# Where the low-rank adapters of eight experts are multiplied out: beside the attention scores instead of between other products and in the expert stage

## The chip, the cores and the metric

The kernel runs on one core of a Trainium2 chip. The metric is the device time of one execution in microseconds. The times are medians over several runs; a profile is one further execution, recorded by the hardware profiler.

## The reference

The input is 8 sequences of 512 tokens, 512 wide, in float32. Two layers follow each other, each with attention, a residual and a normalisation, then a feed-forward part, a residual and a normalisation. Only the first layer matters here, and of its feed-forward part the expert weights with their adapters:

```python
# layer 0, attention: 16 heads of 32, causal softmax
scores = jnp.einsum('bhqd,bhkd->bhqk', q, k) * (1.0 / math.sqrt(HD))
attn = jax.nn.softmax(jnp.where(causal, -jnp.inf, scores), axis=-1)
...
# layer 0, feed-forward: 8 experts (E), 2 of them for each token, adapters of rank R = 16
gup = jnp.einsum('th,eho->teo', xf, gate_up_proj)
gup = gup + SCALING * jnp.einsum('ter,eor->teo', jnp.einsum('th,erh->ter', xf, gup_lora_A), gup_lora_B)
gates, h = jnp.split(gup, 2, axis=-1)
h = jax.nn.silu(gates) * h
out = jnp.einsum('tei,eih->teh', h, down_proj)
out = out + SCALING * jnp.einsum('ter,ehr->teh', jnp.einsum('tei,eri->ter', h, down_lora_A), down_lora_B)
```

The adapters need not be applied to the tokens. Before and after, the kernel adds `SCALING * A^T B` to the expert's weights once and uses the sum.

## The kernel before, in words

An expert has six chunks of weights of 128 x 512 (`UPS`): four of gate and up, two of down. All eight experts lie in one SBUF tensor, `experts`. While attention of the first layer runs, the places of experts 4 to 7 hold the attention's own weights and the transposed inputs, so only experts 0 to 3 are loaded early; 4 to 7 follow in the last batch and behind it. The adapters of four experts lie in one tile `lora`, each expert in its own group of 32 partitions, of which 16 are used; the second four take the same tile later.

Attention goes over the batches b = 0 to 7, in each over four groups g of four heads, and in each group over three units u: score columns for key tile 0 (u = 0), key tiles 1 and 3 (u = 1), key tile 2 (u = 2). `scores(b, g, u)` multiplies q and k into the score tile `sc` (4 PSUM banks of 128 x 512, one buffer), ScalarE takes the exponential into `p`, and GpSimd masks the diagonal blocks (`affine_select`). In unit 2 only 256 of each bank's 512 columns are used. One unit later `product` multiplies `p` with the values into `av`, and VectorE adds `p` to the row sums (the line `tensor_tensor(total...)`). A group later, in u = 1, `normalise` sums over the keys (`rs`), takes the reciprocal on VectorE and lets GpSimd add it to a guard (`watch_inverses`, into `g_total`).

Everything else of attention (values, queries, keys, the output projection `ps_o`, the router's logits and choice) is hung between the units by `plan(b)`, as a list of thunks for each (g, u). They share two PSUM banks, the tag `mm`, in turn. The order of instructions on each engine is made by a scheduler at build time from its own estimates; in the last batch from g = 2 on, and in the expert stage's beginning, TensorE's order is the order of the program text. GpSimd also adds a row of biases to the inputs x once per batch (`x + row`), which the scheduler puts near groups 2 and 3.

`merge()` takes the next of 24 steps (e, c), for the experts e and e + 1 and the chunk c. `Experts.merge` multiplies the two deltas (16 rows of contraction, 128 x 512 each) into two `mm` banks named `ps_lora`, ScalarE scales them into `scaled` (two buffers, shared with the reciprocal's tile), and GpSimd adds them to the weights. `plan` places two merges in each of the batches 1 to 6, at (2, 2) and (3, 2) once the block transposes are done by DMA. That makes experts 0 to 3. The other twelve stand behind attention, between the steps of `Tiles` (one step is one tile of 128 tokens through one expert: `gate_up`, `turn_hidden`, `down`), where project, score, choose, dispatch, one_hot and enter of the last batch are placed too.

Of the kernel before, what the change touches and what calls it, by code (L numbers as in the profile page):

```python
# [9 lines left out]
F32 = mybir.dt.float32  # L10
# [4 lines left out]
ALU = mybir.AluOpType  # L15
# [3 lines left out]
P = 128  # L19
NB = 8  # L20
S = 512
D = 512
NT = S // P
ND = D // P
# [734 lines left out]
class Experts:  # L759

    def __init__(self, env, pool):
        self.env, self.nc = env, env.nc
        self.w = pool.tile([P, E * EXPERT], F32, name="experts")
        self.by_expert = self.w.rearrange("p (e f) -> p e f", f=EXPERT)

# [4 lines left out]

    def load(self, e):
        at = e * EXPERT
        for src, n in ((self.env.ins.gate_up[e], ND), (self.env.ins.down[e], UPS - ND)):
            self.nc.sync.dma_start(out=self.w[:, at : at + n * 512].rearrange("p (u f) -> p u f", f=512),
                                   in_=src.rearrange("u p f -> p u f"))
            at += n * 512
# [4 lines left out]
        for j in range(4):  # L783
            self.nc.sync.dma_start(out=self.lora[32 * j : 32 * j + R, :], in_=self.env.ins.lora[i, j])

    def delta(self, ps, e, c):
        j = 32 * (e % 4)
        a, bt = lora_factors(self.lora[j : j + R, :], c)
        self.nc.tensor.matmul(ps, lhsT=a, rhs=bt, start=True, stop=True)

    def chunk(self, e, c, n=1):
        return self.by_expert[:, e : e + n, 512 * c : 512 * (c + 1)]

    def merge(self, e, c, ps, scaled):


        for i in range(2):
            self.delta(ps[i], e + i, c)
        for i in range(2):
            self.nc.scalar.mul(scaled[i], ps[i], LORA_SCALE)  # L800
            w = self.chunk(e + i, c)[:, 0, :]
            self.nc.gpsimd.tensor_tensor(w, w, scaled[i], ALU.add)


class Tiles:
# [425 lines left out]
def attention0(env, guard, keep, routes, experts, dram, p_mm, tiles_ctx):  # L1231
# [8 lines left out]
    with ExitStack() as phase:  # L1240
# [151 lines left out]
        def scores(b, g, u):  # L1392
            q, k = heads[b, g]
            sc = p_sc.tile([P, 4, S], F32, tag="sc", name="sc")
            width = 0
            for kt in UNITS[u]:
                w = S - P * kt
                for j in range(4):
                    hs = slice(HD * j, HD * (j + 1))
                    matmul_by_columns(nc, sc[:, j, width : width + w], k[hs, ts(kt, P)], q[hs, P * kt :], columns=64)  # L1400
                width += w
            p = own.tile([P, 4, width], F32, tag=f"p{u}", name="p", bufs=2 if u == 0 else 1)
            nc.scalar.activation(p, sc[:, :, :width], AF.Exp, scale=scale)  # L1403

            at = 0
            for kt in UNITS[u]:
                first = p[:, :, at : at + P]
                nc.gpsimd.affine_select(out=first, in_=first, pattern=[[0, 4], [1, P]], compare_op=ALU.is_ge, fill=0.0,  # L1408
                                        base=0, channel_multiplier=-1)
                at += S - P * kt  # L1410
            return p

        def product(b, g, u, p, acc):
# [28 lines left out]
            nc.vector.tensor_tensor(aoTs[b][:, g, :], av, r_inv, ALU.mult)  # L1442
            guard.watch_inverses(r_inv)

        merges = [(e, c) for e in range(0, E, 2) for c in range(UPS)]

        def merge(n=1):
            for _ in range(min(n, len(merges))):
                e, c = merges.pop(0)
                ps = [mm([P, 512], "ps_lora") for _ in range(2)]  # L1450
                experts.merge(e, c, ps, [work.tile([P, 512], F32, tag="r_inv", name="scaled", bufs=2) for _ in ps])

        def plan(b):

            todo, late = ({(g, u): [] for g in range(ND) for u in range(len(UNITS))} for _ in range(2))
            for slot, places in (((0, 0), (0, 1)), ((0, 1), (3,)), ((0, 2), (2,))):
                todo[slot] += [lambda t=t: value(b, t) for t in places]
            pb, last = b - 1, b == NB - 1
            by_dma = 0 <= pb < by_blocks
            for g in range(ND):  # L1460
                nb, ng = (b, g + 1) if g + 1 < ND else (b + 1, 0)
                if nb < NB:
                    todo[g, 0 if by_dma and ng == 0 else 1].append(lambda nb=nb, ng=ng: query(nb, ng))
                    todo[g, 1 if by_dma and ng == 0 else 2].append(lambda nb=nb, ng=ng: key(nb, ng))
            if b:
                places = ((1, 0), (1, 1), (1, 2), (2, 0)) if by_dma else ((1, 0), (1, 0), (1, 1), (1, 1) if last else (1, 2))
                for t, slot in enumerate(places):
                    todo[slot].append(lambda t=t: project(pb, t))
                if by_dma:
                    todo[2, 1].append(lambda: blocks(pb))  # L1470
                else:
                    for c in range(ND):
                        at = todo[2, 1] if last and c >= 2 else (late if last else todo)[2, 0]
                        at.insert(c % 2 if at is todo[2, 1] else len(at), lambda c=c: turn(pb, c))
                todo[(3, 2) if by_dma else (2, 1)].append(lambda: score(pb))
                if not by_dma:
                    todo[2, 2].append(lambda: choose(pb))
                if not last:
                    todo[2, 2 if by_dma else 1].append(merge)
                    todo[3, 2 if by_dma else 1].insert(0, merge)  # L1480
            if b == 0:
                todo[1, 0].append(lambda: router.merge_lora(mm([P, ND, E], "ps_wr")))
            if b > 1:
                todo[0, 0].append(lambda: choose(b - 2))
                todo[1, 0].append(lambda: dispatch(b - 2))
                todo[1, 2].append(lambda: enter(one_hot(b - 2, range(NT))))
            if last:
                todo[1, 2].append(soon)
                todo[2, 2].append(first_rows)
                late[3, 1].append(first_turned)  # L1490
                todo[3, 2] += [begin, lambda: dispatch(b - 1)]
            return todo, late
# [25 lines left out]
        for b in range(NB):  # L1518
            todo, late = plan(b)
            for g in range(ND):  # L1520
                if g == 2:
                    if b + 1 < NB:
                        load_xT(b + 1)

                    nc.gpsimd.tensor_tensor(xs[b], xs[b], row[:, 1:2, :].to_broadcast([P, NT, D]), ALU.add)
                if g == 3 and b + 1 < NB:
                    load_x(b + 1)
                if b == NB - 1 and g == 1:
                    experts.load_lora(work, 1)
                    experts.load(4)  # L1530
                if b == NB - 1 and g == 2:
                    order.enter_context(in_order(tc))
                if b == NB - 1 and g == 3:
                    experts.load(5)
                    experts.load(6)
                acc = []
                for u in range(len(UNITS)):
                    p = scores(b, g, u)
                    for thunk in todo[g, u]:
                        thunk()  # L1540
                    begun.close()
                    if waiting is not None:
                        waiting()
                    for thunk in late[g, u]:
                        thunk()
                    if u == 1 and summing is not None:
                        summing()
                    waiting = lambda b=b, g=g, u=u, p=p, acc=acc: product(b, g, u, p, acc)
                summing = lambda b=b, g=g, acc=acc: normalise(b, g, acc)
        waiting()  # L1550
        summing()
        merge()
        heads_ctx.close()
        tiles.open(tiles_ctx)
        tiles.step(merge)
        b = NB - 1
        one_hot(b - 1, (0, 1))
        project(b, 0, True)
# [5 lines left out]
        enter(rows, columns=P)  # L1564
        for _ in range(2):
            tiles.step()
            merge()
        for c in range(ND):
            turn(b, c, mm if c in (1, 2) else tiles.aside)
        tiles.step()  # L1570
        score(b)
        merge()
        choose(b, P)
        tiles.step()
        merge()
        dispatch(b, tiles.aside, P)
        for places in ((0, 1), (2, 3)):
            rows = one_hot(b, places)
            tiles.step()
            merge()  # L1580
        enter(rows, tiles.aside, P)
        tiles.of_fixed = router.fixed(routes)
        while merges:
            tiles.step()
            merge()
        order.close()
    return router, tiles, router.tables(routes, p_mm.tile([P, E], F32, tag="mm", name="ps_count"), guard.routed[:, 1:2])

# [289 lines left out]
def usual_pass(tc, ins, held_out):  # L1878
    nc = tc.nc
    with ExitStack() as ctx:  # L1880
# [4 lines left out]
        with tc.tile_pool(name="a_mm", bufs=2, space=PSUM) as p_mm, ExitStack() as attn1_ctx:  # L1885
            with tc.tile_pool(name="routes", bufs=1, side="right") as routes, \
                    tc.tile_pool(name="experts", bufs=1, side="right") as pool, ExitStack() as tiles_ctx:
                experts = Experts(env, pool)
                router, tiles, tables = attention0(env, guard, keep, routes, experts, dram, p_mm, tiles_ctx)

                def load_rows(b):
# [335 lines left out]
```

## Time and profile before

| | |
|---|---|
| median of 3 runs | 2159.9 us (2158.47 to 2159.97) |
| profiled execution | 2158.07 us, of which the span of instructions is 2156.4 us |
| mean granted TensorE clock | 0.997 |
| TensorE busy | 2121.3 us (98% of the span) |
| VectorE busy | 1280.0 us (59%) |
| ScalarE busy | 628.8 us (29%) |
| GpSimd busy | 495.0 us (23%) |
| attention of layer 0 | about the first 700 us of the span |
| expert tiles | from about 696 us to about 1150 us |

Busy time counts an engine's instructions, not its waits. Work on the other engines counts only where TensorE ends up waiting for it. In a timeline a line has the start in us, the length, the engine, the line of the kernel, the operation, what it writes and reads, how often it came in a row, and in brackets the idle time before it with what ended it. A float32 product appears as two records, one for each pass.

### The profile page before, as it was taken

The page shows a single profiled execution, that of the slowest core. Times are in us where ns is not written, and L with a number is a line of the kernel's source. Part 1 is how long each engine was busy: PE and PEld are TensorE (multiplying, and loading weights), DVE is VectorE, ACT ScalarE, POOL GpSimd, SP SyncE. Part 2 cuts the span into 40 slices and gives each one's busy share as a digit, 9 for nine tenths or more (in the row PEclk, how much of TensorE's full clock was granted, in tenths as well). Part 3 has the DMA queues.
Part 4 walks back from the last instruction along what each step waited for, and adds up shares of the span by engine and source line. Part 5 has one row for each costly group of instructions (what it writes and reads, how often), then busy time and mean ns, then how long its engine had stood idle before and what let it go on. Part 6 is the DMA issues. An engine that isn't in the chain of part 4 may idle for free. (4 is left out here: it accounts for less than half of the span.)

```text
span 2156.4 us, 35260 instructions
## 1 busy us (share of the span) xinstructions
PE 2121.3 (98%) x14746; PEld 996.3 (46%) x14746; DVE 1280.0 (59%) x2042; ACT 628.8 (29%) x907; POOL 495.0 (23%) x489
## 2 busy tenths in 40 slices
PE   9999999999998999999999999999999999999997
PEld 2333333333333444444443333333334888888886
DVE  2657676776767544224326988889857644555443
ACT  2332323323323221122124333332332232222222
POOL 2333414424233342132014222232211000000000
PEclk9999999999999999999999999999999999999999
DMA  9030312303222228797644121331201311111000
GB/s 308 21 95 6 99 30 71 99 2 98 71 68 89 98 91 231 214 234 195 193 157 139 57 87 55 98 98 40 79 1 45 103 59 59 59 59 59 20 20 21
DMA packets 160010, 195.53 MB, mean 91 GB/s; under 512 B 61010, under 2 KB 101970, under 8 KB 157282
## 3 DMA queue, kind: packets, MB, share of 16 engines
q1 hardware_dynamic: 148560, 157.49, 23.8%
q0 software_dynamic: 10560, 34.61, 5.6%
q8 instruction: 119, 1.95, 0.4%
q10 hardware_dynamic: 722, 1.07, 0.1%
q14 instruction: 49, 0.40, 0.1%
HBM read 123.67 MB, written 69.47 MB: 90 GB/s over the span
## 5 line engine op out<-in xcount | busy, mean ns | idle before, releaser
L911 PE MATMUL ps_gu<-experts,xrT 128*128 128x512 f32 (+1 forms) x520 | 247.4, 598 | 0.0
L1403 ACT ACTIVATE p<-sc 128x2048 f32<-128x2048 f32 (+1 forms) x96 | 153.1, 1595 | 144.8 <-PE sc L62 121.1
L1165 DVE SCALAR_TENSOR_TENSOR hT<-ps_u,vec,sg 128x512 f32<-128x512 f32 x88 | 65.6, 746 | 189.4 <-PE ps_u L1160 189.4
L1176 PE MATMUL ps_f<-ffn_w,h_half 128*128 128x512 f32 x672 | 169.7, 393 | 2.7 <-DVE h_half L1171 2.0
L1015 POOL TENSOR_TENSOR g_total<-g_total,r_inv 128x512 f32<-128x512 f32 x64 | 90.0, 1406 | 352.4 <-DVE r_inv L1788 270.2
L1408 POOL TENSOR_SCALAR_AFFINE_SELECT p<-p 128x512 f32<-128x512 f32 x128 | 90.2, 717 | 341.0 <-ACT p L1403 303.5
L1431 DVE TENSOR_TENSOR p<-p 128x1536 f32<-128x1536 f32 (+2 forms) x96 | 139.3, 1451 | 44.6 <-POOL p L1408 41.2
L1758 ACT ACTIVATE p<-sc 128x1024 f32<-128x1024 f32 x128 | 124.1, 1022 | 99.0 <-PE sc L62 98.9
L913 DVE TENSOR_TENSOR h<-ps_gu,h 128x256 f32<-128x256 f32 x67 | 28.5, 425 | 207.0 <-ACT h L912 207.0
L1788 DVE RECIPROCAL r_inv<-r_inv 128x512 f32<-128x512 f32 x32 | 107.1, 3346 | 68.5 <-ACT r_inv L1012 68.5
L1176 PEld LDWEIGHTS ps_f<-ffn_w,h_half 128*128 128x128 f32 x672 | 124.4, 188 | 34.9 <-DVE h_half L1171 7.7
L1160 PE MATMUL ps_g<-x_high,ffn_w 128*128 128x512 f32 x352 | 137.2, 390 | 0.9 <-DVE x L1730 0.9
L1160 PE MATMUL ps_g<-x_low,ffn_w 128*128 128x512 f32 x352 | 137.0, 389 | 0.0
L911 PEld LDWEIGHTS ps_gu<-experts,xrT 128*128 128x128 f32 x520 | 95.6, 196 | 89.5 <-issue 89.2
L1160 PE MATMUL ps_u<-x_high,ffn_w 128*128 128x512 f32 x352 | 136.9, 389 | 0.0
L1160 PE MATMUL ps_u<-x_low,ffn_w 128*128 128x512 f32 x352 | 136.9, 389 | 0.0
L927 PE MATMUL ps_y<-experts,hT 128*128 128x512 f32 (+1 forms) x272 | 128.0, 593 | 0.5 <-ACT hT L921 0.5
L62 PE MATMUL ps_q<-experts 128*32 128x512 f32 x1024 | 121.9, 605 | 4.9 <-DMA experts<-in_xT 4.6
L62 PE MATMUL sc<-qT,kT 64*64 64x512 f32 x1024 | 124.7, 602 | 1.1 <-ACT qT L1664 0.7
L1777 PE MATMUL av<-p,v 128*64 128x512 f32 x512 | 120.9, 593 | 0.0
L62 PE MATMUL ps_o<-attn_out,aoT 128*64 128x512 f32 x512 | 116.4, 598 | 0.8 <-ACT r_inv L1012 0.8
L62 PE MATMUL ps_k<-experts 128*32 128x512 f32 x1024 | 116.3, 594 | 0.0
(269 smaller groups left out, 3275.8 us busy)
## 6 DMA issues: line engine op xcount, KB each, us to landing
results<-y SPq DMA_DIRECT2D x68, 256.0 KB, 2.2
turned<-turned SPq DMA_DIRECT2D x56, 256.0 KB, 4.1
pair<-xrT SPq DMA_DIRECT2D x25, 512.0 KB, 3.1
xrT<-pair SPq DMA_DIRECT2D x100, 128.0 KB, 4.5
x<-in_x SPq DMA_DIRECT2D x8, 1024.0 KB, 8.3
experts<-in_gate_up SPq DMA_DIRECT2D x8, 1024.0 KB, 11.4
rows<-x SPq DMA_DIRECT2D x32, 256.0 KB, 2.3
x<-rows SPq DMA_DIRECT2D x8, 1024.0 KB, 15.4
```

What stands on the lines that cost most here:

```text
L62: nc.tensor.matmul(out[m], lhsT=lhsT[:, m], rhs=rhs, start=start, stop=stop)
L911: nc.tensor.matmul(ps, lhsT=xT[:, c, :], rhs=self.weights(i, c), start=c == 0, stop=c == ND - 1)
L927: self.nc.tensor.matmul(ps, lhsT=hT[:, c, :], rhs=self.weights(i, ND + c), start=c == 0, stop=c == self.NI - 1)
L1015: self.nc.gpsimd.tensor_tensor(self.total, self.total, r_inv, ALU.add)
L1160: nc.tensor.matmul(ps, lhsT=w[:, ts(dc, P)], rhs=x[:, dc, :], start=(dc, i) == (0, 0), stop=(dc, i) == (ND - 1, 1))
L1176: self.nc.tensor.matmul(os[t], lhsT=h[:, ts(t, P)], rhs=self.weights(2 * NHID + c), start=(c, i) == (0, 0), stop=(c, i) == (NHID - 1, 1))
L1403: nc.scalar.activation(p, sc[:, :, :width], AF.Exp, scale=scale)
L1408: nc.gpsimd.affine_select(out=first, in_=first, pattern=[[0, 4], [1, P]], compare_op=ALU.is_ge, fill=0.0, base=0, channel_multiplier=-1)
L1431: nc.vector.tensor_tensor(total[:, :, P * kt :], total[:, :, P * kt :], p[:, :, at : at + w], ALU.add)
L1758: nc.scalar.activation(p, sc, AF.Exp, scale=scale)
L1777: nc.tensor.matmul(st["av"][HD * j : HD * (j + 1), :], lhsT=st["v"][:, kt, HD * j : HD * (j + 1)], rhs=p[:, j, :], start=kt == 0, stop=kt ...
L1788: nc.vector.reciprocal(r_inv, r_inv)
```

## The change

1. The deltas are made four experts at a time, for one chunk's half (256 columns), in columns of 64: eight small products per time. They are written into the 256 columns of each bank of `sc` that unit 2 does not use, just ahead of unit 2's scores. This is done in all four groups of batches 1 to 6, 24 times. Batches 1 to 3 make experts 0 to 3, batches 4 to 6 make experts 4 to 7.
2. ScalarE scales them two experts at a time, straight behind the exponential, into tiles of their own. GpSimd's add follows one unit later for the first pair and two units later for the second.
3. For experts 4 to 7 the weights' half chunks are loaded for this purpose, added to, and stored to a DRAM tensor `merged`. In the last batch and behind it, those experts are loaded from `merged`, one transfer each.
4. The second adapters are loaded at the start of batch 4 instead of in batch 7.
5. All calls of `merge` go. The loop at the end that ran a step for each merge left now runs until twelve steps are done.
6. The area for descriptors of GpSimd's own DMAs is set to 8192 bytes a partition.

```diff
+    def deltas(self, ps, c, half):
+        for e in range(4):
+            a, bt = lora_factors(self.lora[32 * e : 32 * e + R, :], c)
+            matmul_by_columns(self.nc, ps[:, e, :], a, bt[:, 256 * half : 256 * (half + 1)], columns=64)
+    def pair(self, ps, i, k, own):
+        nc = self.nc
+        second, c, half = k // 12, k % 12 // 2, k % 2
+        e, f = 2 * i, slice(512 * c + 256 * half, 512 * c + 256 * (half + 1))
+        scaled = own.tile([P, 2, 256], F32, tag=f"scaled{i}", name="scaled")
+        nc.scalar.mul(scaled, ps[:, e : e + 2, :], LORA_SCALE)
+        if not second:
+            w = self.by_expert[:, e : e + 2, f]
+            return {1 + i: lambda: nc.gpsimd.tensor_tensor(w, w, scaled, ALU.add)}
+        w = []
+        def load():
+            w.append(own.tile([P, 2, 256], F32, tag=f"merged{i}", name="merged"))
+            ins, u = self.env.ins, c if c < ND else c - ND
+            src = (ins.gate_up if c < ND else ins.down)[4 + e : 6 + e, u, :, 256 * half : 256 * (half + 1)]
+            nc.sync.dma_start(out=w[0], in_=src.rearrange("e p f -> p e f"))
+        return {i: load, 1 + i: lambda: nc.gpsimd.tensor_tensor(w[0], w[0], scaled, ALU.add),
+                2 + i: lambda: nc.sync.dma_start(out=self.merged[:, e : e + 2, f], in_=w[0])}
...
     def load(self, e):
         at = e * EXPERT
+        if e >= 4:
+            self.nc.sync.dma_start(out=self.by_expert[:, e, :], in_=self.merged[:, e - 4, :])
+            return
...
         def scores(b, g, u):
             q, k = heads[b, g]
             sc = p_sc.tile([P, 4, S], F32, tag="sc", name="sc")
+            free = sc[:, :, S - 256 :]
+            beside = ND * (b - 1) + g if u == 2 and 0 < b < NB - 1 else None
+            if beside is not None:
+                experts.deltas(free, beside % 12 // 2, beside % 2)
...
             nc.scalar.activation(p, sc[:, :, :width], AF.Exp, scale=scale)
+            n = len(UNITS) * (ND * b + g) + u
+            if beside is not None:
+                for i in range(2):
+                    for after, thunk in experts.pair(free, i, beside, own).items():
+                        merging.setdefault(n + after, []).append(thunk)
...
+            for thunk in merging.pop(n, []):
+                thunk()
             return p
...
-                if not last:
-                    todo[2, 2 if by_dma else 1].append(merge)
-                    todo[3, 2 if by_dma else 1].insert(0, merge)
...
+                if b == NB // 2 and g == 0:
+                    experts.load_lora(work, 1)
                 if b == NB - 1 and g == 1:
-                    experts.load_lora(work, 1)
                     experts.load(4)
...
-        while merges:
+        while tiles.next < 12:
             tiles.step()
-            merge()
...
-    nc = bacc.Bacc("TRN2", target_bir_lowering=False, num_devices=1)
+    nc = bacc.Bacc("TRN2", target_bir_lowering=False, num_devices=1, dynamic_dma_scratch_size=8192)
```

More of the change, by code (lines that the diff above doesn't have):

```diff
@@ L759, with __init__ @@
 class Experts:
-    def __init__(self, env, pool):
+    def __init__(self, env, pool, dram):
         self.env, self.nc = env, env.nc
+        self.merged = dram.tile([P, 4, EXPERT], F32, name="merged")
         self.w = pool.tile([P, E * EXPERT], F32, name="experts")
@@ L784, in load_lora @@
             self.nc.sync.dma_start(out=self.lora[32 * j : 32 * j + R, :], in_=self.env.ins.lora[i, j])
[L786 to L802, printed above, removed]
+    def deltas(self, ps, c, half):
[19 more added lines that the diff above has]
+                2 + i: lambda: nc.sync.dma_start(out=self.merged[:, e : e + 2, f], in_=w[0])}
 class Tiles:
@@ L1443, in normalise @@
             guard.watch_inverses(r_inv)
[L1445 to L1451, printed above, removed]
+        merging = {}
         def plan(b):
@@ L1551, in attention0 @@
         summing()
-        merge()
         heads_ctx.close()
         tiles.open(tiles_ctx)
-        tiles.step(merge)
+        tiles.step()
         b = NB - 1
@@ L1566, in attention0 @@
             tiles.step()
-            merge()
         for c in range(ND):
@@ L1571, in attention0 @@
         score(b)
-        merge()
         choose(b, P)
         tiles.step()
-        merge()
         dispatch(b, tiles.aside, P)
@@ L1579, in attention0 @@
             tiles.step()
-            merge()
         enter(rows, tiles.aside, P)
         tiles.of_fixed = router.fixed(routes)
-        while merges:
+        while tiles.next < 12:
             tiles.step()
-            merge()
         order.close()
@@ L1887, in usual_pass @@
                     tc.tile_pool(name="experts", bufs=1, side="right") as pool, ExitStack() as tiles_ctx:
-                experts = Experts(env, pool)
+                experts = Experts(env, pool, dram)
                 router, tiles, tables = attention0(env, guard, keep, routes, experts, dram, p_mm, tiles_ctx)
```

## The prediction

> **What bounds the kernel now.** I read the page's busy table first, then the answers on the tile ps_lora (the products of the adapters, which the change moves), then the timelines of TensorE, VectorE and GpSimd around the places where they stand.
>
> ```profile
> PE 2121.3 (98%) x14746; PEld 996.3 (46%) x14746; DVE 1280.0 (59%) x2042; ACT 628.8 (29%) x907; POOL 495.0 (23%) x489
> L789 PE MATMUL ps_lora<-lora x96: 587/640/692, 148.6 to 799.6; 16*128 16x512 f32 x96
> 140.00:700.00 560.00, 22.69 (x52) 7.60 (x52) 14.94 (x25) 1.00 0.22 70
> 700.00:820.00 120.00, 13.16 (x44) 3.58 (x44) 12.76 (x23) 0.99 0.33 109
> ```
>
> TensorE is busy for 98% of the span, so time is won only where its own work goes or where one of its waits goes. The 96 records are 48 products, two passes each. The last two lines are that tile's busy time (PE, weight load, ACT): 22.69 us in the attention batches, 13.16 us in the tail (experts' first tiles). So at most about 36 us is at stake. The seam between two batches, on TensorE (start, length, group, idle before it):
>
> ```profile
> 249.54 0.69 PE L62 MATMUL sc<-q,k 32*64 32x256 f32 x16
> 250.16 1.44 PE L789 MATMUL ps_lora<-lora 16*128 16x512 f32 x4
> 252.03 1.06 PE L498 MATMUL ps_logits<-x1T,r_wr 128*32 128x512 f32 x8 [0.43 <-ACT scaled L800]
> 252.91 1.05 PE L1423 MATMUL av<-p,v 128*32 128x384 f32 x16
> 253.88 1.11 PE L62 MATMUL sc<-q,k 32*64 32x512 f32 x16
> 254.93 7.07 PE L62 MATMUL ps_v<-experts 128*32 128x512 f32 x64
> 261.82 0.44 PE L62 MATMUL ps_r<-r_gather,logits 128*32 128x8 f32 x31
> ```
>
> A merge of two products costs 252.03 - 250.16 = 1.87 us of TensorE here, a wait of 0.43 us on ScalarE in it. The other engines at the same seam:
>
> ```profile
> 245.14 4.57 POOL L1525 TENSOR_TENSOR x<-x,row 128x2048 f32<-128x2048 f32 x1 [0.99 <-issue]
> 251.42 1.57 POOL L1408 TENSOR_SCALAR_AFFINE_SELECT p<-p 128x512 f32<-128x512 f32 x1 [0.53 <-ACT p L1403]
> 255.91 1.54 POOL L1015 TENSOR_TENSOR g_total<-g_total,r_inv 128x512 f32<-128x512 f32 x1 [1.67 <-DVE r_inv L1441]
> 257.40 2.26 POOL L802 TENSOR_TENSOR experts<-experts,scaled 128x512 f32<-128x512 f32 x1
> 252.43 3.34 DVE L1441 RECIPROCAL r_inv<-r_inv 128x512 f32<-128x512 f32 x1
> 256.83 1.70 DVE L1431 TENSOR_TENSOR p<-p 128x1024 f32<-128x1024 f32 x1
> 258.64 0.69 DVE L1307 TENSOR_TENSOR v<-ps_v,row 128x512 f32<-128x512 f32 x1
> ```
>
> See that unit 2's mask (251.42) comes before g_total, that VectorE's sum of that unit (256.83) is long since free to run, and that the first v leaves its bank (258.64 to 259.33) 2.5 us before ps_r, which takes that bank, starts at 261.82.
>
> **Removed in the batches.** Each of batches 1 to 6 has two merges: 1.87 us above, and 237.16 - 235.23 = 1.93 us in group 2. 6 x 3.80 = 22.8 us. Two waits of ps_v on ScalarE's scaled copy go too (1.3 us in the list of waits). Together -24.1 us.
>
> **Added in the batches.** 24 times, eight products of 16 x 64 by 16 x 256, written to the half of the score tile that unit 2 leaves unused. The trace has no such group, but sc of unit 2 has the same number of instructions, column halves, width, row groups and banks: 250.16 - 249.54 = 0.62 us. I assume 16 rows are no quicker than 32, and two row groups do overlap with 16 rows: a ps_lora merge takes 1.06 us in the tail (702.14 to 703.20) against 1.93 us where it can't. Bounds 0.6 and, if only two ran at once, 16 records at about 0.24 us over 2, 1.9 us. I take 0.62: 24 x 0.62 = +14.9 us.
>
> **Waits that the change makes.** The order built for each engine shows two.
> (1) Score tile. It has one buffer; its release now waits for exp (1.02 us) and two scaled copies (1.09 us the pair, 0.60 us each). I set before and after equal at the start of rs in group 2 (230.07). After: sc of unit 2 in group 3 starts at 248.73, ends 249.42, exp 249.52, copies end 251.65, sc of the next batch may start about 251.85. TensorE's own work until then (logits 0.88, av 0.98, one v instruction 0.22) ends at 251.43. Wait 0.42 us. In groups 0 to 2 a key (3.46) and av (0.98) stand there: hidden.
> (2) GpSimd's order. The new order puts g_total ahead of unit 2's mask, and both adds right behind that mask. g_total waits for VectorE's reciprocal, so the mask slips behind it. At the seam: reciprocal ends 255.7, g_total 257.35, mask (0.63) 258.0, first add (1.27) 259.25, then VectorE's sum (1.15 undisturbed: 256.83 plus 1.70, less the wait for g_total's end at 257.4), v's evacuation at 260.5 to 261.2. ps_r would start at 251.85 + 1.05 + 6.68 = 259.58. Wait about 1.6 us.
>
> Does the sum wait for one add, for both, or for none? Row: the add at 257.40 takes 2.26 us and not 1.27, since the sum was waiting when g_total ended and went first. [...] If VectorE won at once it would be 0.35 us; if it lost twice, 2.9 us. [...]
>
> In groups 0 to 2 the same slip has cover: o needs v's bank at 196.0 and gets it at about 195.7; o in group 1 at 221.3, about 220.1; in group 2 the mask is done at 240.7 and its av starts at 241.2. These are thin, 0.3 to 1.2 us. x + row (245.14) waits for its load and in batch 4 came 1.3 us later; that goes straight into the seam: +1.3 us once. Sum of waits: 6 x 2.0 + 1.3 = +13.3 us. Ends: 6 x 0 and 6 x 4.2.
>
> **Batches:** -24.1 + 14.9 + 13.3 = +4.1 us.
>
> **The tail.** Twelve merges go: 1.99 (696.30), ten of 1.06, 1.87 (744.09): 14.46 us, and 0.15 us of ps_x1T on scaled. But the merge at 744.09 hid ScalarE's copy of the logits:
>
> ```profile
> 743.10 1.06 PE L498 MATMUL ps_logits<-x1T,r_wr 128*32 128x512 f32 x8
> 744.09 1.90 PE L789 MATMUL ps_lora<-lora 16*128 16x512 f32 x4
> 745.96 1.06 PE L62 MATMUL ps_r<-r_gather,logits 128*128 128x8 f32 x8
> 746.87 3.66 PE L911 MATMUL ps_gu<-experts,xrT 128*128 128x512 f32 x4
> 745.00:750.00 5.00, 5.00 (x15) 0.70 0.18 52
> ```
>
> The copy ends at 744.82, so ps_r now waits 0.86 us. The next late thing would be the last project: its VectorE chain (one-hots) was held for 4.33 us by GpSimd's g_total and two adds; without the adds it ends near 708, ps_o needs its bank at 709. -14.6 + 0.86 = -13.75 us.
>
> The last line is the granted clock: 0.70 over these 5 us, and the four ps_gu at 746.87 took 3.66 instead of 1.88 us. TensorE was never idle; 3.8 us of thin products stood before. [...]
>
> **Edits taken at nothing.** 48 transfers of 256 KB on SP's queue (24 loads, 24 stores) and the second adapters' load moved from batch 7 to 4: SP mostly waits for VectorE's normalised rows, the DMA engines are 0.17 to 0.26 busy there, and the adapters have a unit of 20 us. A late store would hold x's load behind it, at the price of the batch-4 case: 0 to 1.3 us a batch in 4 to 6. Experts 4 to 7 now come in one load each; needed at tile 12. The smaller descriptor area: no row shows it; an indirect DMA takes GpSimd 0.96 us and is issued five tiles ahead; 0 to 3 us, I take 0.
>
> **Sum.** +4.1 - 13.75 - 1.75 = -11.4 us against the profiled execution's 2158.07 us (its span is 2156.4): 2146.7. The median of the runs, 2159.9, is 1.8 us above that execution: 2148.
>
> **Rivals.**
> - No new waits (0.14): VectorE wins its turns and the score tile is free in time. -24.1 + 14.9 - 15.5 = -24.7: 2135. For it: GpSimd is 23% busy. Against: the order on GpSimd.
> - Slower, the adds hold VectorE (0.10): both adds go ahead of each sum. Then o in group 0 waits 0.9 us, ps_r 2.9, the score tile 0.42, and thin covers in groups 1 and 2 about 0.8: 5.0 a batch, 30 us instead of 13.3, and the dip stays: 2148 + 16.9 + 1.75 = 2167. It decides from (24.1 - 14.9 + 15.5)/6 = 4.1 us a batch on. For it: the 4.33 us row, where VectorE lost twice running. Against: in all twelve adds behind a g_total VectorE went first.
> - The change doesn't do what it says (0.06): the eight products don't overlap, 1.9 instead of 0.62 us, 24 x 1.28 = 31 us more: 2179.
>
> **How the numbers follow.** The forecast has 0.70, with 2141 to 2156 as its own range. With the rivals, 2137 to 2158 leaves about 2 in 10 out. A measurement of this kernel tells 0.2% (4.3 us, so 2155.6 and 2164.2) from no change. Faster: 0.14 and nine tenths of 0.70, about 0.78; same: the rest of 0.70 and a share of the slower rival, 0.11; slower: 0.11.
>
> **What would show it.** Right: no ps_lora; sc groups from lora of 0.62 us; at each seam sc waits about 0.4 us on ScalarE and ps_r 1 to 2 us on VectorE; in the tail steps of 5.8 instead of 7.06 us; clock 1.00 after ps_logits. Wrong: lora groups above 1 us; waits above 4 us a batch; a late x; stalls of TensorE after 850 us.

## The result, and the profile after

The changed kernel takes 2143.07 us (median of 6 runs, 2142.19 to 2145.68), the kernel before 2159.87 us in the same session. The ratio is 0.9928, 95% interval 0.9918 to 0.9938: faster by 16.8 us, where 11.4 to 11.9 us were forecast (2148, range 2137 to 2158). The profiled execution is the longest of the six (2145.68 us, span 2143.9) and the one of before lay 1.8 us under its median, so the two traces differ by 12.5 us in span. The reckoning below is one of traces; the differences of medians stand beside it.

The page's busy line, and the answer on the tile lora (the products that took the place of ps_lora):

```profile
PE 2099.9 (98%) x15034; PEld 992.5 (46%) x15034; DVE 1283.9 (60%) x2042; ACT 627.3 (29%) x907; POOL 498.1 (23%) x489
L62 PE MATMUL sc<-lora x384: 374/400/426, 100.1 to 597.3; 16*64 16x256 f32 x192
```

TensorE has more instructions and is busy for 21 us less. The timeline of TensorE at the seam that was shown of before (start, length, group, and in brackets the idle time ahead of it and who ended it):

```profile
247.92 1.04 PE L1462 MATMUL rs<-p,ones 128*32 128x512 f32 x8
248.89 0.69 PE L62 MATMUL sc<-lora 16*64 16x256 f32 x16
249.38 0.64 PE L62 MATMUL sc<-q,k 32*64 32x256 f32 x16
249.94 1.07 PE L498 MATMUL ps_logits<-x1T,r_wr 128*32 128x512 f32 x8
252.57 1.07 PE L1447 MATMUL av<-p,v 128*32 128x384 f32 x16 [1.56 <-POOL p L1430]
253.46 1.02 PE L62 MATMUL ps_v<-experts 128*32 128x512 f32 x2
254.41 1.11 PE L62 MATMUL sc<-q,k 32*64 32x512 f32 x16
255.46 7.07 PE L62 MATMUL ps_v<-experts 128*32 128x512 f32 x62
263.24 0.44 PE L62 MATMUL ps_r<-r_gather,logits 128*32 128x8 f32 x32 [0.72 <-DVE v L1320]
```

Four things are to be seen.

- The group of lora delays the scores behind it by 249.38 - 248.89 = 0.49 us, not 0.62.
- ps_r waits for VectorE as forecast, but 0.72 us (six times, 4.3 us in the list of waits), not 1.6.
- av, which was ready to run in the forecast, waits 1.56 us for a mask on GpSimd: five times, 4.7 us in all.
- The score tile's wait on ScalarE does not appear. Two records of ps_v, the two passes of one product, stand ahead of the next scores instead, and this is not free: by themselves they hold TensorE for 254.41 - 253.46 = 0.95 us, and the 62 behind them take 7.07 us, as the 64 did before.

GpSimd and VectorE at the same place:

```profile
247.37 4.56 POOL L1540 TENSOR_TENSOR x<-x,row 128x2048 f32<-128x2048 f32 x1 [2.08 <-DMA x<-in_x]
251.86 1.24 POOL L1430 TENSOR_SCALAR_AFFINE_SELECT p<-p 128x512 f32<-128x512 f32 x2
258.13 1.54 POOL L1028 TENSOR_TENSOR g_total<-g_total,r_inv 128x512 f32<-128x512 f32 x1 [5.02 <-DVE r_inv L1465]
259.62 0.63 POOL L1430 TENSOR_SCALAR_AFFINE_SELECT p<-p 128x512 f32<-128x512 f32 x1
260.23 3.49 POOL L805 TENSOR_TENSOR experts<-experts,scaled 128x512 f32<-128x512 f32 x2
252.55 2.17 DVE L1455 TENSOR_TENSOR p<-p 128x1536 f32<-128x1536 f32 x1 [8.34 <-POOL p L1430]
254.64 3.34 DVE L1465 RECIPROCAL r_inv<-r_inv 128x512 f32<-128x512 f32 x1
260.28 2.30 DVE L1455 TENSOR_TENSOR p<-p 128x1024 f32<-128x1024 f32 x1 [1.17 <-POOL p L1430]
```

x + row begins when x has landed, holds GpSimd until 251.9, and only then come the two masks that av waits for (252.57). The sum behind unit 2's mask takes 2.30 us, where the prediction reckoned 1.15 for the sum alone and one add of 1.27 ahead of it: that part is as forecast.

TensorE in the tail, and a window of 5 us (the granted clock is the number after the five engines' busy times, here 1.00):

```profile
731.82 2.10 PE L1374 MATMUL ps_x1T<-ident,x 128*128 128x128 f32 x16 [0.94 <-DVE xrT L900]
...
739.65 1.06 PE L498 MATMUL ps_logits<-x1T,r_wr 128*32 128x512 f32 x8
741.43 1.06 PE L62 MATMUL ps_r<-r_gather,logits 128*128 128x8 f32 x8 [0.71 <-ACT logits L1387]
742.34 1.96 PE L924 MATMUL ps_gu<-experts,xrT 128*128 128x512 f32 x4
...
749.34 0.41 PE L62 MATMUL ps_rank<-both,r_before 128*128 128x32 f32 x2 [0.94 <-DVE xrT L900]
...
762.61 1.91 PE L62 MATMUL ps_table<-one_hot 128*128 128x256 bf16 x16 [0.94 <-DVE xrT L900]
745.00:750.00 5.00, 4.06 (x16) 2.11 (x15) 3.65 (x18) 1.67 (x2) 0.00 (x0) 1.00 0.09 35
```

The clock is 1.00 behind ps_logits and the four ps_gu take 1.96 us: the dip is gone. ps_r waits 0.71 us, as reckoned. Three waits of 0.94 us are new and were not forecast: ps_x1T, ps_rank and ps_table use the bank of the ps_xrT just before them, and a merge used to stand between.

By anchors in the two traces: up to ps_r of the last batch (675.72 before, 676.93 after) the change loses 1.2 us; from there to the end (1480.6 against 1466.9 us) it gains 13.7.

### The profile page after: what moved, and what is told of

It reads as the page before. It is cut to its first block, busy times and chain, and to the rows that moved or that the text cites. A ratio compares the mean times of both kernels' runs of the same rounds, so it can differ in the third digit from the quotient of the medians.

```text
span 2143.9 us, 35859 instructions
## 1 busy us (share of the span) xinstructions
PE 2099.9 (98%) x15034; PEld 992.5 (46%) x15034; DVE 1283.9 (60%) x2042; ACT 627.3 (29%) x907; POOL 498.1 (23%) x489
## 5 line engine op out<-in xcount | busy, mean ns | idle before, releaser
L1455 DVE TENSOR_TENSOR p<-p 128x1536 f32<-128x1536 f32 (+2 forms) x96 | 149.3, 1555 | 80.6 <-POOL p L1430 77.5
L62 PE MATMUL ps_v<-experts 128*32 128x512 f32 x1024 | 120.9, 594 | 0.0
L1430 POOL TENSOR_SCALAR_AFFINE_SELECT p<-p 128x512 f32<-128x512 f32 x128 | 81.5, 649 | 165.3 <-ACT p L1420 158.7
```

The lines of the kernel that those rows point to most:

```text
L62: nc.tensor.matmul(out[m], lhsT=lhsT[:, m], rhs=rhs, start=start, stop=stop)
L1455: nc.vector.tensor_tensor(total[:, :, P * kt :], total[:, :, P * kt :], p[:, :, at : at + w], ALU.add)
```

## The experiments

All ratios are to the kernel before, run beside them. "Period" is the length of a batch in the profiled execution: the mean of the five distances between the six starts of ps_logits between about 160 and 605 us (the six seams).

| kernel | median us | ratio (95%) | period us |
|---|---|---|---|
| before | 2159.87 | 1 | 86.87 |
| changed | 2143.07 | 0.9928 (0.9918 to 0.9938) | 87.06 |
| tail_left_out | 2142.67 | 0.9927 (0.9913 to 0.9941) | 86.66 |
| nothing_merged | 2127.11 | 0.9858 (0.9843 to 0.9873) | 83.89 |
| products_only | 2140.12 | 0.9911 (0.9896 to 0.9926) | 86.07 |
| no_adds | 2138.42 | 0.9906 (0.9891 to 0.9921) | 85.85 |
| x_row_moved | 2147.01 | 0.9943 (0.9929 to 0.9956) | 88.53 |
| x_row_in_reciprocal | 2142.73 | 0.9930 (0.9917 to 0.9944) | 85.59 |
| before_x_moved | 2158.48 | 1.0000 (0.9991 to 1.0009) | 86.59 |
| tail_banks | 2139.78 | 0.9911 (0.9898 to 0.9925) | 86.98 |
| both_moves | 2138.62 | 0.9906 (0.9891 to 0.9921) | 85.63 |
| both_moves_2 | 2133.89 | 0.9889 (0.9874 to 0.9904) | 85.58 |

### Where the gain sits: tail_left_out

```diff
 # in the kernel before
                 e, c = merges.pop(0)
+                if len(merges) < 12:
+                    return
                 ps = [mm([P, 512], "ps_lora") for _ in range(2)]
```

> The kernel before, with the twelve merges of the tail left out (half of the adapters are then not added); the batches are untouched. It tells how the gain divides. Theory T (the tail made all of it): from the profiled executions the tail is 13.7 us shorter after the change and the batches 1.2 us longer, so this kernel should take 13 to 15 us off the kernel before (about 2146 us, ratio 0.9935), with three new waits of ps_x1T, ps_rank and ps_table on VectorE's copy of the turned rows (0.94 us each), one of ps_r on ScalarE's logits (0.7 us), and the granted clock at 1.00 after ps_logits. Rival B (the batches gave part of it): the medians differ by 16.8 us where the profiled executions differ by 12.4; if the rest sits in the tail, 17 us or more come off here, and if the batches gave 3 us, 13 to 14 come off.

It took 2142.67 us, 16 us under the before of its session (2158.63) and level with the changed kernel: the gain is the tail's, and the batches give about nothing. In the trace the stretch from the last batch's ps_r to the end is 1466.6 us, 14.0 less than before, with the same three waits of 0.94 us and the clock at 1.00 from 735 to 750. Theory T. The interval of the ratio is 12.7 to 18.8 us, so a few us from the batches (rival B) are not excluded by the medians; the periods, 86.66 here and 87.06 in the changed kernel, speak against any.

### What the parts cost in the batches: nothing_merged, products_only, no_adds

```diff
 # nothing_merged: no products, and none of the rest
-            if beside is not None:
-                experts.deltas(free, beside % 12 // 2, beside % 2)
 # nothing_merged and products_only: no copies, adds, transfers
-            if beside is not None:
-                for i in range(2):
-                    for after, thunk in experts.pair(free, i, beside, own).items():
-                        merging.setdefault(n + after, []).append(thunk)
         # in load(): experts 4 to 7 come from gate_up and down, as in the kernel before
 # no_adds
-            return {1 + i: lambda: nc.gpsimd.tensor_tensor(w, w, scaled, ALU.add)}
+            return {}
-        return {i: load, 1 + i: lambda: nc.gpsimd.tensor_tensor(w[0], w[0], scaled, ALU.add),
-                2 + i: lambda: nc.sync.dma_start(...)}
+        return {i: load, 2 + i: lambda: nc.sync.dma_start(...)}
```

> The changed kernel without the merging: no products, copies, adds or transfers of merged weights (the adapters are not added). Against products_only it prices the 24 groups of eight products. By the trace a group delays what follows by 0.48 us: 24 x 0.48 = 11.5 us, of which those at the seams may be hidden in the wait of av; so 9 to 12 us less than products_only, about 2127 us. The prediction had 0.62 us each, 14.9 us. Rival: products of 16 rows run wholly beside the scores: no difference.

> The changed kernel with the 24 groups of adapter products in the score tile alone: no scaled copies, no adds, no load or store of merged weights (the adapters are not added). Against the run without adds it tells what the two scaled copies cost through the score tile's release. Theory S of the prediction (release late by 0.42 us at each seam): 2 to 3 us less than without adds, about 2136 us. Rival (hidden, since av waits there longer or as long): no difference, 2138 us; the transfers of merged weights delaying x would show here too, as less wait of av on the mask in batches 4 to 6.

> The changed kernel without its 48 adds on GpSimd (the adapters are then not added; products, scaled copies, loads and stores stay). Theory A (the first add holds VectorE's sum behind the mask): the sum of unit 2 takes 1.15 us instead of 2.30 at each seam, the first v leaves its bank 1.15 us earlier and the wait of ps_r (0.72 us) goes: 4 to 5 us less than the changed kernel, about 2139 us. Theory X (x + row sets the seam): the same for ps_r, but av's wait on the mask stays at 0.4 to 1.6 us in the seams. [...]

From nothing_merged to products_only the period grows by 86.07 - 83.89 = 2.18 us, four groups at 0.55; 13.0 us in the medians. Copies and transfers of merged weights add nothing on balance (85.85 - 86.07 = -0.22): the rival of theory S. But this is a balance of two things. In no_adds, as in the changed kernel, the two records of ps_v stand ahead of the next scores and cost 0.95 us a seam; in products_only they do not, so the late release of the score tile shows as another order and not as a wait. In their place ps_r waits for VectorE at each of the six seams of products_only, 5.3 us in all, with no add on GpSimd:

```profile
253.05 7.07 PE L62 MATMUL ps_v<-experts 128*32 128x512 f32 x64
261.00 0.44 PE L62 MATMUL ps_r<-r_gather,logits 128*32 128x8 f32 x32 [0.88 <-DVE v L1317]
```

The adds bring 87.06 - 85.85 = 1.21 us; 4.7 us in the medians, as theory A had it. VectorE and TensorE at the seam of no_adds:

```profile
257.99 1.63 DVE L1454 TENSOR_TENSOR p<-p 128x1024 f32<-128x1024 f32 x1 [1.16 <-POOL p L1429]
259.54 1.44 DVE L1319 TENSOR_TENSOR v<-ps_v,row 128x512 f32<-128x512 f32 x2
250.28 1.07 PE L1446 MATMUL av<-p,v 128*32 128x384 f32 x16 [0.79 <-POOL p L1429]
260.27 0.44 PE L62 MATMUL ps_r<-r_gather,logits 128*32 128x8 f32 x32
```

The sum takes 1.63 instead of 2.30 us and ps_r no longer waits. av still waits for the mask, but less: 1.1 us in two seams instead of 4.7 in five. So A and X do not divide the two waits between them. Both waits hang on one chain: x + row, masks, VectorE's sum and reciprocal, g_total, mask, sum, v. The adds make it longer, x + row makes it start late, and taking away either is enough for ps_r: it no longer waits in x_row_moved (below), with all adds in place. (Part of av's wait also differs from one execution to the next: tail_banks below, with the same attention, has 2.9 us of it.)

The surprise is nothing_merged. Taking the two merges out of a batch of tail_left_out saves 86.66 - 83.89 = 2.8 us, not the 3.8 us that they took. The list of waits of nothing_merged says where the rest went (us in all, times, the longest):

```profile
PE av L1438 <- POOL p L1421: 6.1, 6, 1.3
```

With nothing at all in the merge's place av waits for the mask at every seam. So this wait is not made by what the change adds; it appears when the merge goes. Nor is it made by the changed order on GpSimd: here unit 2's mask runs ahead of g_total, as before.

### Who holds the masks: x_row_moved, x_row_in_reciprocal, before_x_moved

```diff
 # x_row_moved
-                    nc.gpsimd.tensor_tensor(xs[b], xs[b], row[:, 1:2, :].to_broadcast([P, NT, D]), ALU.add)
                     p = scores(b, g, u)
+                    if (g, u) == (1, 0):
+                        token = row[:, 1, 0:1]
+                        nc.vector.scalar_tensor_tensor(out=token, in0=p[:, 0, 0:1], scalar=0.0, in1=token, ...)
+                        for t in range(NT):
+                            nc.gpsimd.tensor_tensor(xs[b][:, t, :], xs[b][:, t, :], row[:, 1, :], ALU.add)
 # x_row_in_reciprocal: the same four adds in normalise() for g == 0, after
+                nc.scalar.activation(token, guard.sums[:, n : n + 1], AF.Identity, scale=0.0, bias=token)
```

The token (a zero times something that is ready at the wanted time, added to one element of row) only holds the four pieces back.

> The changed kernel, with GpSimd's x + row of each batch (4.56 us, one instruction, which stands between two masks just before the seam as soon as x has landed) held back to the next batch's second group and cut in four pieces. Theory X (GpSimd's x + row sets the seam): the masks of unit 1 at the seam come up to 4 us earlier, TensorE's waits of av on the mask (4.7 us in five seams) go, VectorE's reciprocal comes earlier with them, so ps_r's waits (4.3 us) go as well; seams fall from 14.6 us to about 11.9 on average, 12 to 16 us in all: about 2128 us. Rival A (the two adds between mask and sum set ps_r, as the prediction had it): av's waits go, the seam loses 0.8 us, ps_r still waits 0.7 us or more: 2138 us. Rival N: x lands later or the pieces meet the masks of the other group: no gain or a loss.

The seams (start of rs to start of ps_r) fell from between 13.85 and 15.32 us to 11.82 (the first to 12.39), 11.9 on average as theory X had it, and the waits of av and ps_r are gone from the list. A part of this only changed places: four records of ps_r now start ahead of the last three of ps_v, and the others 0.84 us later:

```profile
348.54 0.27 PE L62 MATMUL ps_r<-r_gather,logits 128*32 128x8 f32 x4
348.95 0.60 PE L62 MATMUL ps_v<-experts 128*32 128x512 f32 x3
349.38 0.42 PE L62 MATMUL ps_r<-r_gather,logits 128*32 128x8 f32 x27
```

And the kernel as a whole gained nothing: the period is 1.5 us longer than in the changed kernel, the median 4 us higher (with its five runs between 2142.77 and 2150.09). The rest of a batch rose from 72.6 to 77.05 us, 3.6 more without those 0.84. VectorE's routing, the wait on TensorE and the windows (clock before the last two columns) of x_row_moved:

```profile
284.17 4.99 POOL L1559 TENSOR_TENSOR x<-x,row 128x512 f32<-128x512 f32 x4 [0.28 <-DVE row L1556]
285.55 1.17 DVE L562 TENSOR_TENSOR mine<-r_part,r_hots 128x32 f32<-128x32 f32 x1
288.11 1.08 DVE L566 CAST rank<-r_ranks 128x8 int32<-128x8 f32 x1
295.33 0.74 DVE L1331 TENSOR_SCALAR q<-ps_q,vec 128x512 f32<-128x512 f32 x1
296.13 1.07 PE L1462 MATMUL rs<-p,ones 128*32 128x512 f32 x8 [1.88 <-DVE q L1331]
298.51 4.94 PE L62 MATMUL ps_k<-experts 128*32 128x512 f32 x32
297.00:300.00 3.00, 3.00 (x44) 0.99 (x44) 3.00 (x3) 2.04 (x4) 0.00 (x0) 0.63 0.02 5
```

Beside the pieces, an operation of VectorE on 128x32 that takes 0.18 us in the changed kernel takes 1.17, and one on 128x8 1.08 instead of 0.17; q leaves its bank late, rs waits 1.88 us, and behind this wait the clock is 0.63, so that ps_k takes 4.94 instead of 3.64 us. The adds were put into a hole of GpSimd that was no hole of VectorE.

> The changed kernel, with x + row (in four pieces) held back until ScalarE has read the row sums in the next batch's second group, so that GpSimd runs it while VectorE computes a reciprocal (3.3 us, one operand) and no longer beside VectorE's routing chain. Theory X (x + row held the seam, and where it was put last it held VectorE's routing, which made rs wait 1.9 us and the TensorE clock drop): seams stay at 11.8 us, the rest of a batch goes back from 77.0 to about 72.6 us, the clock stays at 1.00: 6 x 2.8 = 17 us less than the changed kernel, about 2126 us. Rival (x + row costs some 4 us a batch wherever GpSimd runs it, since VectorE's sums with two operands wait for it): the rest stays above 75 us and the time near 2145 us.

The seams stayed at 11.82, rs waited no more, the period fell to 85.59. The rest of a batch (73.8) looks 1.2 us longer, 0.84 of it because of the same change of places at ps_r. Yet the median did not move. At the sixth ps_r (600.95) the trace is 9.8 us ahead of the changed kernel's (610.75); the last batch takes 5.9 of them back (72.1 us to the next ps_r against 66.2), and its ps_x1T waits 4.2 us for VectorE instead of 1.6. That x + row's place in that batch did it is what both_moves_2 shows below. The other 4 us are still there at the end of the trace (span 2140.4 against 2143.9) but not in the medians; the changed kernel's traced execution was the longest of its six.

> The kernel before with x + row held back in the same way as in both_moves_2 and nothing else. It tells whether the merge at the seam had covered x + row. Theory C (it had: TensorE spent the 1.87 us of the merge while GpSimd ran x + row and the masks behind it, so before nothing of it was on the path): the seams fall from 13.5 us only to 13.25, 0 to 3 us less in all, about 2157 us, or a loss where x + row now holds VectorE. Rival (x + row cost the kernel before as much as the changed one): 9 us or more less, below 2150 us.

The edit of both_moves_2 (below), without its tail, in the kernel before: ratio 1.0000, interval 0.9991 to 1.0009, all six seams 13.25 us. In the kernel before x + row cost nothing but its late arrivals, and the same edit is worth about 1.5 us a batch in the changed one. Together with nothing_merged this shows that the merges had covered x + row: theory C. Both of a batch's merges seem to have had a part in it: the merge at the seam held av back, and the one in group 2 held rs back while x + row waited for its own load. At the seam shown x + row starts 248.57 - 245.14 = 3.4 us ahead of rs in the kernel before, 1.5 us in nothing_merged and 0.55 us (247.92 - 247.37) in the changed kernel.

### The tail's new waits, and a better kernel: tail_banks, both_moves, both_moves_2

```diff
-            turn(b, c, mm if c in (1, 2) else tiles.aside)
+            turn(b, c, tiles.aside if c == 2 else mm)
-        dispatch(b, tiles.aside, P)
+        dispatch(b, mm, P)
-        enter(rows, tiles.aside, P)
+        enter(rows, columns=P)
```

> The changed kernel, with three products of the tail in the other pool of PSUM banks (the first ps_x1T, ps_rank and ps_table), so that they do not ask for the bank of the ps_xrT just before them. Theory W (each of them waited 0.94 us for VectorE's copy of ps_xrT, which a merge had hidden before): three waits go, 2.8 us less than the changed kernel, about 2140 us. Rival: the products then wait for the bank's earlier user or the next ps_xrT waits for ps_x1T, and nothing is gained.

It took 2139.78 us, 3 us less; the three waits left the list. TensorE in tail_banks, in the place of the second one:

```profile
744.06 0.60 PE L899 MATMUL ps_xrT<-ident,xr 128*128 128x128 f32 x4
744.50 0.31 PE L62 MATMUL ps_rank<-both,r_before 128*128 128x32 f32 x2
```

> The changed kernel with both moves: x + row held back as in x_row_in_reciprocal, and the three products of the tail in the other bank pool as in tail_banks. If the two are independent the gains add up: 17 us of the seams and 3 us of the tail, about 2123 us, 36 us below the kernel before. Rival: if x + row costs the same wherever it runs, only the tail's 3 us are left, about 2140 us.

2138.62 us: the tail's gain and about 1 us more, the last batch (71.3 us) being nearly as long as in x_row_in_reciprocal. The expected sum was missed for that reason, and both_moves_2 mends it:

```diff
 # x + row in normalise()
-            if g == 0:
+            if g == 0 and b < NB - 1:
 # and for the last batch where x_row_moved had it
+                    if (b, g, u) == (NB - 1, 1, 0):
```

> As both_moves, but in the last batch x + row is held back to the place of x_row_moved (ahead of VectorE's reciprocal) and not to that of x_row_in_reciprocal, where the last batch took 72.05 us against 66.18 and ps_x1T waited 4.2 us on VectorE. Theory X: batches 1 to 6 stay 1.5 us shorter each than in the changed kernel, the last batch comes back to about 67 us, the tail keeps its 3 us: about 2130 us. Rival (the last batch loses the time whatever x + row does): 2138 us again.

2133.89 us, ratio 0.9889 (0.9874 to 0.9904), 3.9 us over the expectation and the fastest complete kernel of the study: 24.5 us below the before of its session, against 16.8 of the change. The last batch is back at 67.0 us (600.93 to 667.92). Its seam:

```profile
333.81 0.64 PE L62 MATMUL sc<-q,k 32*64 32x256 f32 x16
334.38 1.06 PE L498 MATMUL ps_logits<-x1T,r_wr 128*32 128x512 f32 x8
335.26 1.05 PE L1447 MATMUL av<-p,v 128*32 128x384 f32 x16
336.12 1.02 PE L62 MATMUL ps_v<-experts 128*32 128x512 f32 x2
```

No wait between the scores and av, nor at ps_r. The copies, the products and both adds are all still there, and GpSimd's order behind g_total is the same. The two records of ps_v, 0.95 us a seam, are there too; whether they could be saved here was not tried.

### The clock: fill_thin and fill_full

```diff
         score(b)
+        fill = mm([P, 512], "ps_fill")
+        a, bt = lora_factors(experts.lora[0:R, :], 0)
+        for _ in range(2):     # fill_full: range(4), lhsT=experts.w[:, 0:P], rhs=experts.w[:, 0:512]
+            nc.tensor.matmul(fill, lhsT=a, rhs=bt, start=True, stop=True)
         choose(b, P)
```

> The changed kernel with two products of 16 rows (four records, about 1.9 us) put between ps_logits and ps_r of the last batch, written to a spare bank and read by nobody: the thin stretch ahead of the experts' ps_gu is about as long as in the kernel before again. [...] Rival (the dip was not of the stretch's length): clock 1.00, and the fill costs its 1.9 us less the wait of ps_r (0.7 us) and no more.

> As fill_thin, with four products of 128 rows and 512 columns in the place of the thin ones (about 1.7 us). Theory G (what counts is that the rows of TensorE are filled): clock 1.00, four ps_gu in 1.9 us, so fill_full differs from fill_thin although both last as long. [...]

The timeline of TensorE and two windows of fill_thin, then of fill_full:

```profile
739.63 1.98 PE L1589 MATMUL ps_fill<-lora 16*128 16x512 f32 x4
742.45 2.75 PE L924 MATMUL ps_gu<-experts,xrT 128*128 128x512 f32 x4
745.42 2.62 PE L924 MATMUL ps_gu<-experts,xrT 128*128 128x512 f32 x4
740.00:745.00 5.00, 5.00 (x17) 2.22 (x16) 1.80 (x10) 1.86 (x3) 0.00 (x0) 0.85 0.28 88
745.00:750.00 5.00, 5.00 (x15) 2.55 (x13) 2.73 (x18) 2.04 (x3) 0.00 (x0) 0.81 0.00 0
```

```profile
738.71 3.70 PE L1588 MATMUL ps_fill<-experts 128*128 128x512 f32 x8
743.05 1.96 PE L924 MATMUL ps_gu<-experts,xrT 128*128 128x512 f32 x4
740.00:745.00 5.00, 5.00 (x20) 2.70 (x19) 1.30 (x7) 0.96 (x2) 0.00 (x0) 1.00 0.12 44
```

With 1.9 us of thin products the dip is back (two groups of 2.75 and 2.62 instead of 1.96 and 1.88, 1.5 us more, where it cost 1.7 before). The full products took twice the time expected (3.5 us, eight records), and there was none (clock 1.00, 1.96 and 1.88 us). (The whole kernels took 2146.56 and 2146.36 us, one run each.) So 3.5 us of full products between ps_logits and ps_r left the clock at 1.00, and 1.9 us of thin ones went with 0.85 and 0.81: this is as theory G of fill_full has it. With one execution of each, and fills of different length, it is support and not proof.

## Why the prediction was right, and which terms were off

- **The sign and the mechanism.** Right: the tail carries the gain, the batches give about nothing. The sum was -11.4 us against the profiled execution, the traces differ by -12.5. The other 4 us of the medians' 16.8 lie between executions of one kernel, and what makes these differ was not settled; the landing of x (x + row waited 0.65 to 2.08 us for it in batches 1 to 6 of the changed kernel's trace) and a clock dip near 680 us (below) vary from trace to trace.
- **Removed in the batches, -24.1.** This is the step that failed. The products themselves did go, but the sum took it that nothing else would be due at the seam. By the periods the two merges were worth 2.77 x 6 = 16.6 us, by the medians 15.6. The difference is av's wait for the mask, put at nothing: 6.1 us in nothing_merged, 4.7 in the changed kernel. The merges had covered x + row and the masks behind it, and the prediction's line of x + row at 245.14 was read only for its late landing in batch 4.
- **Added, +14.9.** By the periods 2.18 x 6 = +13.1. This has a change of waits in it (av less, ps_r more); in the timeline a group of 16 rows delays what follows by 0.48 to 0.49 us and not 0.62 (assumed no quicker than 32 rows), 24 x 0.49 = 11.8 us.
- **New waits, +13.3.** (1) The score tile, 0.42 us. What came was the order with two records of ps_v ahead of the scores. The prediction had them there and counted them at 0.22 us, their share of a full run; alone they cost 0.95. That no_adds is no slower than products_only is because ps_r waits about as long in the latter. (2) Mask, one add, sum, v, ps_r: right in every link. That the sum would wait for one add, and not for none or two, was the author's estimate, which no run of before shows; in the changed kernel that sum took 2.30 us, against 1.63 in no_adds and the 1.27 + 1.15 of the prediction for one add and the sum. The wait of ps_r was 0.72 us instead of 1.6, in part because TensorE itself, with those 0.95 us, came later to ps_r. The adds as a whole cost 1.21 x 6 = 7.3 us by the periods, 4.7 by the medians.
- **Sum of the batches, +4.1.** Measured +1.2 by the anchors to the kernel before, +2.4 by the periods from tail_left_out. That it came out near is luck: the merges were worth 7.5 us less than counted, and products and waits together about 9 us less.
- **The tail, -13.75, and the clock, -1.75.** Together -15.5; measured -13.7. A step became shorter by 7.06 - 5.81 = 1.25 us and not by the merge's 1.06; the wait of ps_r was right (0.71 for 0.86). Missed were the three waits of 0.94 us, 2.8 us, worth 3 us in tail_banks. The prediction named ps_o as the next late thing; these were nearer, and visible in the program: the same bank as the ps_xrT before. The dip went as forecast: 746.87 to 750.34 were 3.47 us, 742.34 to 744.14 are 1.80, so -1.67. That it would go was the author's estimate, and no run of before shows the -1.75 us. What the runs show: behind a thin stretch from ps_logits to ps_gu of 3.8 us there was a dip, before (743.10 to 746.87, clock 0.70) and in fill_thin (738.63 to 742.45, clock 0.85 and 0.81), and behind one of 2.7 us in the changed kernel (739.65 to 742.34, clock 1.00) there was none. That the thin products bring the dip and not the delay is what fill_thin and fill_full speak for, in one execution each.
- **Edits at nothing.** Transfers and copies together: no cost on balance from products_only to no_adds. The descriptor area was not tried by itself.
- **The rivals.** "No new waits" missed av's wait, ps_r's, and the price of the two records of ps_v. "The adds hold VectorE" needed 4.1 us a batch; the adds cost 1.2. The products do overlap: the 16 records of a group, of 0.40 us each (median), delay what follows by 0.49 us.

## What to carry to other kernels

Before a piece of work on the bounding engine is counted as a gain, list what the other engines run during it: what it covered comes out as a new wait, here 7 of the 24 us taken out of the batches and nearly 3 us in the tail. A wait that an instruction causes is cured by moving that instruction, but the hole it is moved to must be free on every engine that it slows, not only on its own: in x_row_moved GpSimd was free and VectorE was not (an operation of 0.18 us took 1.17). Measure with one part taken out at a time: a sum can be right while its two largest terms are off in opposite directions.

## What the runs showed of the hardware

- Beside four GpSimd adds of 128x512, an operation of VectorE on 128x32 took 1.17 us instead of 0.18, and one on 128x8 1.08 instead of 0.17 (x_row_moved against the changed kernel).
- Two records of ps_v that stood alone held TensorE for 0.95 us, where 64 in a row take 7.07, on average 0.22 for two. A record by itself is 0.59 us long, so those of a row overlap.
- The clock went down with no idle TensorE: before, 745 to 750 us, TensorE was busy for 5.00 of 5.00 us and the clock at 0.70. In fill_thin, with 1.9 us of products with 16 rows, it was 0.85 (740 to 745 us) and 0.81 (745 to 750), in fill_full, with 3.5 us of products with 128 rows, 1.00 in both. In x_row_moved it was 0.63 (297 to 300 us) behind a wait of 1.9 us that was followed by 1.0 us of rs and 0.5 us of lora products.
- A dip near 680 us came in the changed kernel (0.89) and not in tail_banks (1.00), although the program there is the same. The windows from 675 to 690 us, changed kernel and tail_banks:

```profile
675.00:690.00 15.00, 11.98 (x169) 4.78 (x161) 12.21 (x34) 5.94 (x8) 3.80 (x5) 0.89 0.43 163
675.00:690.00 15.00, 11.98 (x160) 4.99 (x153) 13.53 (x34) 8.13 (x9) 4.05 (x5) 1.00 0.31 115
```

Why is open; the same instructions start 2 us earlier in the second.
